# Second attention in program order on TensorE: conv steps between its parts, half of the values' products behind the transposes, both halves copied by ACT

## Chip, core and metric

The kernel runs on one core of a Trainium2 chip. The metric is the device time of one execution in microseconds (us). The engines are TensorE (PE, matrix products; PEld is its weight load), VectorE (DVE), ScalarE (ACT), GpSimd (POOL) and SyncE (SP, which here only issues DMAs). Each engine runs its own queue of instructions in order; semaphores tie the queues together.

## The reference

Two layers on x of shape 2 x 256 x 64 x 64, each with a group norm ahead of it and a residual sum. Layer 0 is an attention with 8 heads over all 4096 positions. Layer 1 is a two-stage block attention plus a 3 x 3 convolution. The part of layer 1 that matters here is its second attention with the sum of both branches:

```
qx = _bn_relu(_c1x1(_bn_relu(_c1x1(feats, fq1_w), ...), fq2_w), ...)
kx = _bn_relu(_c1x1(_bn_relu(_c1x1(feats, fk1_w), ...), fk2_w), ...)
vx = _c1x1(feats, fv_w)
ctx2 = _sa(qx, kx, vx, 8, 8)          # softmax over the 64 positions of a block, 64 blocks
feats2 = _bn_relu(_c1x1(ctx2, sr_W_w), ...)
out = x + rate1 * feats2 + rate2 * conv3x3(...)
```

`_c1x1` is a product with a 256 x 256 matrix over channels, `_bn_relu` a scale and shift per channel with a relu.

## The kernel before, in words

Everything is float32. The two images (b = 0, 1) go one after the other through four stages: projection of layer 0, its attention, the first block attention of layer 1 (tiles named _lr), and `layer1_second`: the second block attention (tiles named _sr) with the convolution woven in. The change is in the last stage and in the helper `group_attention` that the last two share.

An image has NT = 8 tiles of T = 512 positions (8 blocks of 64); its 256 channels are two halves of 128 partitions (KC = 2). For tile t, `layer1_second` does this:

- `branch` for q: two products "ph" (L1075) with relu on ACT into hq (L930), then two products "pr" (`product`, L927) with relu on ACT into rq. The same for k: hk, rk.
- `group_attention`: the scores sp of the 8 blocks (L872), the values vs in two halves of two blocks each (products pvs, L881; half 0 is copied from PSUM by ACT, L886, half 1 by DVE, L888), then the softmax: maximum nm4, difference e, exponential on ACT, sum den, reciprocal and a last multiply (L891 to L898). After a `yield` come two transposes of e into PSUM (at, L903) and two DVE copies into the block-diagonal tile bd (L912); there is one bd for all tiles. After another `yield` come the products pc of vs with bd (L919), handed to ACT for the last relu into res.
- `conv()`, a step of the convolution. There are 16 per image (four strips of 16 rows, four column terms each). A step issues the POOL transform of the *next* step (`conv_transform`: one col, L797, and four v, L801), 16 products into one PSUM tile mm (L811), the ACT copy z of one part of it (L816), four DVE additions that read mm (L817 to L820) and 4 to 12 DVE additions into x (L826 to L838).
- `conv_edges` on DVE (L845), and when a pair of tiles has all its conv steps the final sum with rate1 (L1118) and the store on SP (L1121). Once per image `to_image` copies x into the padded image xp on ACT (L1045), tile by tile ahead of its use, and `fetch_conv_weights` loads the conv weights on SP (L761); for b = 0 it also turns them with 64 transposes (pw, L770), empties the banks with ACT and DVE in turn (L773, L775) and stores them back (L776).

Buffers around the change: PSUM is four banks for all tiles called `bank` and four for the single mm. All work tiles (hq, rq, hk, rk, res, vs, v, z) come from one pool of 11 buffers, given out in the order in which the code asks.

What sets the order: in most stages a scheduler orders each engine's queue by its own estimate, within the data dependences. Inside `with tc.manual_schedule(engines={...})` the named engines keep the order of the program. The first block attention has that for PE; the second does not. There PE's order, as built, is in a steady tile: first piece of ph for q, conv step, rest of ph, pr for q, ph and pr for k, sp and pvs mixed, conv step, at, pc. Each product of 128 x 512 stands in the trace as two pieces ("x8" is four products).

Of the kernel before, what the change touches and what calls it, by code (L numbers as in the profile page):

```python
# [17 lines left out]
P = 128  # L18
B, C, H, W = 2, 256, 64, 64
N = H * W  # L20
T = 512
NT = N // T
KC = C // P
# [8 lines left out]
V_LR, V_FQ1, V_FQ2, V_FK1, V_FK2, V_SRW = (8 + 4 * n for n in range(6))  # L32
# [8 lines left out]
def direct_layers(ctx: ExitStack, tc: tile.TileContext, a: dict, out: bass.AP, bad: bass.AP):  # L41
# [3 lines left out]
    nc = tc.nc  # L45
# [13 lines left out]
    def w4(shape, name, dtype=F32):  # L59
        return work.tile(shape, dtype, tag="w4", name=name)  # L60

    def bank(shape, name):
        return psum["ps"].tile(shape, F32, tag="bank", name=name)
# [29 lines left out]
    for nm, col in (("wk0", V_BK0), ("wq0", V_BQ0)):  # L93
        b0[nm] = const.tile([P, 2], F32, name="b_" + nm)
        for h in range(NH0):
            r = HD0 * (h % 4)
            nc.gpsimd.dma_start(
                out=b0[nm][r : r + HD0, h // 4 : h // 4 + 1],
# [20 lines left out]
    wts = {}  # L119
# [739 lines left out]

    SC1 = C ** -0.5  # L860

    def group_attention(nm, q, k, tokens, wv, out, busy=False):

        sp = bank([P, 4, 64], f"sp_{nm}")
        for t in range(4):
            for c in range(KC):
                for par in range(2):  # L870
                    n0 = (4 * par + t) * 64
                    nc.tensor.matmul(  # L872
                        sp[64 * par : 64 * par + 64, t, :], q[:, c, n0 : n0 + 64], k[:, c, n0 : n0 + 64],
                        start=c == 0, stop=c == KC - 1,
                    )
        vs = w4([P, 4, C], f"vs_{nm}")
        for half in range(2):
            pv = bank([P, 2, C], f"pvs_{nm}_{half}")
            for i in range(2):
                for c in range(KC):  # L880
                    nc.tensor.matmul(  # L881
                        pv[:, i, :], tokens(c, 2 * half + i), wv[:, c, :], start=c == 0, stop=c == KC - 1
                    )
            dst = vs[:, 2 * half : 2 * half + 2, :]
            if half == 0 or busy:
                nc.scalar.copy(dst, pv)  # L886
            else:
                nc.vector.tensor_copy(dst, pv)  # L888

        nm4 = small.tile([P, 4], F32, tag="nm4", name=f"nm4_{nm}")  # L890
        nc.vector.tensor_reduce(nm4, sp, AX.X, ALU.max, negate=True)  # L891
        e = small.tile([P, 4, 64], F32, tag="e", name=f"e_{nm}")
        nc.vector.tensor_tensor(e, sp, nm4.unsqueeze(2).to_broadcast([P, 4, 64]), ALU.add)
        nc.scalar.activation(e, e, AF.Exp, scale=SC1)
        den = small.tile([P, 4], F32, tag="den", name=f"den_{nm}")
        nc.vector.tensor_reduce(den, e, AX.X, ALU.add)
        nc.vector.reciprocal(den, den)
        nc.vector.tensor_tensor(e, e, den.unsqueeze(2).to_broadcast([P, 4, 64]), ALU.mult)  # L898

        yield  # L900
        at = bank([P, 2, 2, 64], f"at_{nm}")
        for u in range(2):
            nc.tensor.transpose(  # L903
                at[:, u].rearrange("p a i -> p (a i)"),
                e[:, 2 * u : 2 * u + 2, :].rearrange("p t j -> p (t j)"), ident,
            )

        bd = bds[turn[0] % 2]
        turn[0] += 1
        for tt in range(2):  # L910
            rows = slice(64 * tt, 64 * tt + 64)
            nc.vector.tensor_copy(  # L912
                bd[rows, :, tt, :].rearrange("p (a u) i -> p u a i", a=2), at[rows]
            )
        yield
        for m in range(KC):
            pc = bank([P, T], f"pc_{nm}_{m}")
            for w in range(4):
                nc.tensor.matmul(  # L919
                    pc[:, w * P : (w + 1) * P], vs[:, w, m * P : (m + 1) * P],  # L920
                    bd[:, w].rearrange("p a i -> p (a i)"), start=True, stop=True,
                )
            out(m, pc)

    def product(pt, wt, src, m, last=True):
        for k in range(KC):
            nc.tensor.matmul(pt, wt[:, k, m * P : (m + 1) * P], src[:, k, :], start=k == 0, stop=last and k == KC - 1)  # L927

    def bn_relu(dst, src, col, m):
        nc.scalar.activation(  # L930
            dst, src, AF.Relu, bias=vecs[:, col + 2 + m : col + 3 + m], scale=vecs[:, col + m : col + m + 1]
        )
# [102 lines left out]
    def layer1_second(b, xts, feats, mean, rstd, shift, pacc):  # L1035

        xp = apool.tile([P, KC, PADW, PADW], F32, tag="A", name=f"xp_{b}")
        for k in range(KC):
            nc.gpsimd.memset(xp[:, k, 0, :], 0.0)
            nc.gpsimd.memset(xp[:, k, PADW - 1, :], 0.0)  # L1040
            nc.gpsimd.memset(xp[:, k, 1 : PADW - 1, 0 : PADW : PADW - 1], 0.0)

        def to_image(t):
            for k in range(KC):
                nc.scalar.activation(  # L1045
                    xp[:, k, 1 + 8 * t : 9 + 8 * t, 1 : 1 + W], xts[t][:, k, :].rearrange("p (r w) -> p r w", w=W),
                    AF.Identity, bias=shift[:, k : k + 1], scale=rstd[:, k : k + 1],
                )

        for t in range(3):  # L1050
            to_image(t)
        results = {}
        turns = [divmod(n, 4) for n in range(4 * NT // 2)]
        ahead = {0: conv_transform(b, xp, *turns[0])}
        done = 0

        def conv():
            nonlocal done
            if done + 1 < len(turns):
                ahead[done + 1] = conv_transform(b, xp, *turns[done + 1])  # L1060
            conv_step(b, xts, wf, ahead.pop(done), *turns[done], pacc)
            done += 1

        for t in range(NT):
            nt = f"sr_{b}_{t}"
            f = [
                feats[k][:, 8 * t : 8 * t + 8].rearrange("p o d e -> p (o d e)") for k in range(KC)
            ]

            def branch(one, two, col1, col2, nm):  # L1070
                hid = w4([P, KC, T], f"h{nm}_{nt}")
                for m in range(KC):
                    ph = bank([P, T], f"ph{nm}_{nt}_{m}")
                    for k in range(KC):
                        nc.tensor.matmul(  # L1075
                            ph, wts[one][:, k, m * P : (m + 1) * P], f[k], start=k == 0, stop=k == KC - 1
                        )
                    bn_relu(hid[:, m, :], ph, col1, m)
                res = w4([P, KC, T], f"r{nm}_{nt}")
                for m in range(KC):  # L1080
                    pr = bank([P, T], f"pr{nm}_{nt}_{m}")
                    product(pr, wts[two], hid, m)
                    bn_relu(res[:, m, :], pr, col2, m)
                return res

            q = branch("fq1", "fq2", V_FQ1, V_FQ2, "q")
            k = branch("fk1", "fk2", V_FK1, V_FK2, "k")
            if t == 0:
                wf = fetch_conv_weights(b)
            for tt in {0: (3, 4)}.get(t, (t + 4,)):  # L1090
                if tt < NT:
                    to_image(tt)
            if t == 0:
                conv()
            res = w4([P, KC, T], f"res_{nt}")

            def to_res(m, pc, res=res):

                bn_relu(
                    res[:, m, :].rearrange("p (d o e) -> p o d e", d=8, o=8),  # L1100
                    pc.rearrange("p (o d e) -> p o d e", o=8, d=8), V_SRW, m,
                )

            parts = group_attention(
                nt, q, k, lambda c, w, f=f: f[c][:, w * P : (w + 1) * P], wts["fv"], to_res
            )
            next(parts)
            conv()
            next(parts)
            if t + 1 < NT:  # L1110
                conv()
            next(parts, None)
            conv_edges(xts, t)
            results[t] = res
            for n in sorted(n for n in results if done >= 4 * (n // 2 + 1)):
                res = results.pop(n)
                for m in range(KC):
                    nc.vector.scalar_tensor_tensor(  # L1118
                        res[:, m, :], res[:, m, :], wts["rate1"], xts[n][:, m, :], ALU.mult, ALU.add
                    )  # L1120
                nc.sync.dma_start(  # L1121
                    out=out[b, :, n * T : (n + 1) * T].rearrange("(k p) n -> p k n", p=P), in_=res
                )
# [583 lines left out]
```

## Time and profile before

| | us |
|---|---|
| median of 3 runs | 3304.72 (3301.09 to 3309.56) |
| the profiled execution | 3297.36, span 3295.2 |
| second attention, image 0, first phq to last pc | 1346.82 to about 1654.2 |
| second attention, image 1, first phq to last pc | 2981.05 to about 3283.7 |
| wait of PE for bd ahead of pc, 16 times | 27.9 in all |

The page gives busy time for each engine, then the span in slices, the chain of work that ended last, and groups of instructions. A group's row reads: line, engine, operation, output <- inputs, shapes, count, busy time, mean time of one, idle time ahead of it and what ended that. A timeline row reads: start, duration, engine, line, operation, output <- inputs, count, and in brackets the idle time ahead of it with its releaser. PE's matmuls are pipelined, so the distance from one start to the next says more than a duration.

### The profile page before, as it was taken

The page shows a single profiled execution, that of the slowest core. Times are in us where ns is not written, and L with a number is a line of the kernel's source. Part 1 is how long each engine was busy: PE and PEld are TensorE (multiplying, and loading weights), DVE is VectorE, ACT ScalarE, POOL GpSimd, SP SyncE. Part 2 cuts the span into 40 slices and gives each one's busy share as a digit, 9 for nine tenths or more (in the row PEclk, how much of TensorE's full clock was granted, in tenths as well). Part 3 has the DMA queues.
Part 4 walks back from the last instruction along what each step waited for, and adds up shares of the span by engine and source line. Part 5 has one row for each costly group of instructions (what it writes and reads, how often), then busy time and mean ns, then how long its engine had stood idle before and what let it go on. Part 6 is the DMA issues. An engine that isn't in the chain of part 4 may idle for free. (4 is left out here: it accounts for less than half of the span.)

```text
span 3295.2 us, 62532 instructions
## 1 busy us (share of the span) xinstructions
PE 3139.2 (95%) x25113; PEld 1844.7 (56%) x25113; DVE 2416.1 (73%) x3138; ACT 2310.7 (70%) x2354; POOL 843.4 (26%) x929
## 2 busy tenths in 40 slices
PE   7999999999999979999979999999999999799998
PEld 4455555555555535666654555555555555356665
DVE  4688888888989888554446887978889898424454
ACT  2798999999989943422227999999999999424222
POOL 2122222223222210444201222222222222005331
PEclk9999999999999979999989999999999999799999
DMA  7967878689776631300159678787797776200000
GB/s 258 251 136 152 168 144 181 145 158 183 143 163 139 141 76 47 134 26 26 45 187 255 137 153 171 142 175 153 158 185 144 156 145 139 79 2 10 14 13 27
DMA packets 243917, 425.23 MB, mean 129 GB/s; under 512 B 99009, under 2 KB 109593, under 8 KB 241185
## 3 DMA queue, kind: packets, MB, share of 16 engines
q0 software_dynamic: 98336, 241.20, 37.8%
q1 hardware_dynamic: 145280, 179.93, 20.5%
q8 instruction: 199, 3.26, 0.4%
q14 instruction: 102, 0.83, 0.1%
HBM read 118.26 MB, written 67.86 MB: 56 GB/s over the span
## 5 line engine op out<-in xcount | busy, mean ns | idle before, releaser
L479 DVE TENSOR_TENSOR e<-e,es 128x1024 f32<-128x1024 f32 (+1 forms) x950 | 1034.4, 1149 | 57.2 <-ACT es L432 57.0
L442 PE MATMUL av<-es,v 128*32 128x256 f32 (+1 forms) x9644 | 745.6, 390 | 0.0
L432 ACT ACTIVATE es<-sa 128x1536 f32<-128x1536 f32 (+1 forms) x444 | 635.6, 1431 | 92.3 <-PE sa L426 47.7
L479 DVE TENSOR_TENSOR e<-e,v 128x1024 f32<-128x1024 f32 (+1 forms) x630 | 668.9, 1118 | 22.7 <-ACT v L432 22.3
L426 PE MATMUL sa<-q,k 128*128 128x512 f32 x1736 | 561.1, 430 | 13.7 <-issue 4.5
L442 PE MATMUL av<-v 128*32 128x256 f32 (+1 forms) x6228 | 506.9, 389 | 0.0
L442 PEld LDWEIGHTS av<-es,v 128*32 128x32 f32 x9644 | 316.2, 109 | 299.4 <-issue 160.2
L426 PEld LDWEIGHTS sa<-q,k 128*128 128x128 f32 x1736 | 279.9, 188 | 297.0 <-issue 139.9
L426 PE MATMUL sc<-q,k 128*128 128x512 f32 x1180 | 373.1, 397 | 7.2 <-ACT es L432 4.3
L426 PE MATMUL sb<-q,k 128*128 128x512 f32 x1180 | 371.3, 396 | 2.1 <-ACT es L432 1.6
L442 PEld LDWEIGHTS av<-v 128*32 128x32 f32 x6228 | 216.3, 109 | 178.5 <-issue 81.5
L432 ACT ACTIVATE es<-sc 128x1024 f32<-128x1024 f32 x296 | 306.8, 1037 | 3.8 <-DVE e L479 3.8
L432 ACT ACTIVATE v<-sc 128x1024 f32<-128x1024 f32 x294 | 304.9, 1037 | 0.4 <-DMA es<-v 0.2
L432 ACT ACTIVATE es<-sb 128x1024 f32<-128x1024 f32 x296 | 302.1, 1021 | 2.9 <-DMA acc<-es 2.9
L432 ACT ACTIVATE v<-sb 128x1024 f32<-128x1024 f32 x294 | 300.1, 1021 | 2.6 <-DMA acc<-v 1.4
L426 PEld LDWEIGHTS sc<-q,k 128*128 128x128 f32 x1180 | 209.0, 187 | 83.6 <-ACT es L432 17.3
L426 PEld LDWEIGHTS sb<-q,k 128*128 128x128 f32 x1180 | 220.2, 188 | 59.0 <-ACT es L432 4.1
L489 POOL DMA_DIRECT2D es<-es x118 | 101.4, 859 | 523.4 <-ACT es L432 468.5
L801 POOL TENSOR_TENSOR v<-col 128x512 f32<-128x512 f32 x128 | 167.0, 1330 | 264.7 <-DMA out_dram<-res_sr 116.9
L432 ACT ACTIVATE v<-sa 128x1536 f32<-128x1536 f32 (+1 forms) x146 | 209.2, 1433 | 33.4 <-PE sa L426 15.2
L811 PE MATMUL mm<-v,wf 128*128 128x256 f32 x1024 | 226.6, 379 | 2.2 <-POOL v L801 1.2
L816 ACT COPY z<-mm 128x512 f32<-128x512 f32 x32 | 18.7, 585 | 283.8 <-PE mm L811 268.3
(241 smaller groups left out, 3519.0 us busy)
## 6 DMA issues: line engine op xcount, KB each, us to landing
acc<-es POOLq DMA_DIRECT2D x122, 512.0 KB, 6.1
acc<-v POOLq DMA_DIRECT2D x76, 512.0 KB, 6.3
es<-es POOLq DMA_DIRECT2D x136, 256.0 KB, 3.8
v<-es POOLq DMA_DIRECT2D x132, 256.0 KB, 4.6
k<-wk_halves SPq DMA_DIRECT2D x64, 512.0 KB
q<-wq_halves SPq DMA_DIRECT2D x256, 128.0 KB
v<-v POOLq DMA_DIRECT2D x92, 256.0 KB, 4.8
es<-v POOLq DMA_DIRECT2D x88, 256.0 KB, 3.8
```

The source lines that it names most:

```text
L426: nc.tensor.matmul(sc[:, i, :], held["k", g // 2][:, j * P : (j + 1) * P], held["q", g, u // 2][:, u % 2, :], start=True, stop=True,)
L432: nc.scalar.activation(dst, sc[:, i : i + m, :], AF.Exp, scale=SC0)
L442: nc.tensor.matmul(dst[HD0 * u : HD0 * u + HD0, n], lhs, rhs(u)[:, n], start=start, stop=stop)
L479: nc.vector.tensor_add(dst[:, s, :], dst[:, s, :], src)
L489: nc.gpsimd.dma_start(out=dst, in_=src, accum_op=ALU.add)
L801: (nc.gpsimd.tensor_add if plus else nc.gpsimd.tensor_sub)(dst, rows(one), rows(two))
L811: nc.tensor.matmul(mm[:, m, r, :], wf[:, k, 4 * r + q, m * P : (m + 1) * P], v[r // 2][:, r % 2, k, :], start=k == 0, stop=k == KC - 1,)
L816: nc.scalar.copy(z[:, 1], mm[:, :, 1, :])
```

## The change

`group_attention` gets a parameter `apart`, set for the second attention alone. With it, half 0 of the values is multiplied ahead of the scores and half 1 behind the transposes and the copies into bd, and ACT copies both. The body of the tile loop goes under `manual_schedule` for PE, in a new order: q branch, image copies, (t = 0: conv weights), conv step, k branch, attention up to the softmax, conv step, transposes with half 1 of the values, pc; at t = 0 a third conv step. In `branch` the second product runs over k outside and m inside, with both banks open.

```
@@ group_attention
+    def group_attention(nm, q, k, tokens, wv, out, busy=False, apart=False):
+        vs = w4([P, 4, C], f"vs_{nm}")
+        def values(half):
+            pv = bank([P, 2, C], f"pvs_{nm}_{half}")
+            for i in range(2):
+                for c in range(KC):
+                    nc.tensor.matmul(
+                        pv[:, i, :], tokens(c, 2 * half + i), wv[:, c, :], start=c == 0, stop=c == KC - 1
+                    )
+            dst = vs[:, 2 * half : 2 * half + 2, :]
+            if half == 0 or busy or apart:
+                nc.scalar.copy(dst, pv)
+            else:
+                nc.vector.tensor_copy(dst, pv)
+        if apart:
+            values(0)
         sp = bank([P, 4, 64], f"sp_{nm}")
...
+        if not apart:
+            values(0)
+            values(1)
...
             nc.vector.tensor_copy(
                 bd[rows, :, tt, :].rearrange("p (a u) i -> p u a i", a=2), at[rows]
             )
+        if apart:
+            values(1)
         yield
@@ layer1_second, branch
+                pr = [bank([P, T], f"pr{nm}_{nt}_{m}") for m in range(KC)]
+                for k in range(KC):
+                    for m in range(KC):
+                        nc.tensor.matmul(
+                            pr[m], wts[two][:, k, m * P : (m + 1) * P], hid[:, k, :], start=k == 0, stop=k == KC - 1
+                        )
                 for m in range(KC):
-                    pr = bank([P, T], f"pr{nm}_{nt}_{m}")
-                    product(pr, wts[two], hid, m)
-                    bn_relu(res[:, m, :], pr, col2, m)
+                    bn_relu(res[:, m, :], pr[m], col2, m)
@@ layer1_second, tile loop
-            q = branch("fq1", "fq2", V_FQ1, V_FQ2, "q")
-            k = branch("fk1", "fk2", V_FK1, V_FK2, "k")
-            if t == 0:
-                wf = fetch_conv_weights(b)
-            for tt in {0: (3, 4)}.get(t, (t + 4,)):
-                if tt < NT:
-                    to_image(tt)
-            if t == 0:
-                conv()
...
-            next(parts)
-            conv()
-            next(parts)
-            if t + 1 < NT:
-                conv()
-            next(parts, None)
+            with tc.manual_schedule(engines={mybir.EngineType.PE}):
+                q = branch("fq1", "fq2", V_FQ1, V_FQ2, "q")
+                for tt in {0: (3, 4)}.get(t, (t + 4,)):
+                    if tt < NT:
+                        to_image(tt)
+                if t == 0:
+                    wf = fetch_conv_weights(b)
+                if t + 1 < NT:
+                    conv()
+                k = branch("fk1", "fk2", V_FK1, V_FK2, "k")
...
+                next(parts)
+                conv()
+                next(parts)
+                next(parts, None)
+                if t == 0:
+                    conv()
```

More of the change, by code (lines that the diff above doesn't have):

```diff
@@ L860, in direct_layers @@
     SC1 = C ** -0.5
-    def group_attention(nm, q, k, tokens, wv, out, busy=False):
+    def group_attention(nm, q, k, tokens, wv, out, busy=False, apart=False):
[14 more added lines that the diff above has]
+            values(0)
         sp = bank([P, 4, 64], f"sp_{nm}")
@@ L875, in group_attention @@
                     )
[L876 to L888, printed above, removed]
+        if not apart:
+            values(0)
+            values(1)
         nm4 = small.tile([P, 4], F32, tag="nm4", name=f"nm4_{nm}")
@@ L1083, in branch @@
-                    bn_relu(res[:, m, :], pr, col2, m)
-                return res
-            q = branch("fq1", "fq2", V_FQ1, V_FQ2, "q")
-            k = branch("fk1", "fk2", V_FK1, V_FK2, "k")
-            if t == 0:
-                wf = fetch_conv_weights(b)
-            for tt in {0: (3, 4)}.get(t, (t + 4,)):
-                if tt < NT:
-                    to_image(tt)
-            if t == 0:
-                conv()
[L1095 to L1102, printed above, removed]
@@ L1104, in layer1_second, with to_res @@
-            parts = group_attention(
-                nt, q, k, lambda c, w, f=f: f[c][:, w * P : (w + 1) * P], wts["fv"], to_res
-            )
-            next(parts)
-            conv()
-            next(parts)
-            if t + 1 < NT:
-                conv()
-            next(parts, None)
+                    bn_relu(res[:, m, :], pr[m], col2, m)
+                return res
+            with tc.manual_schedule(engines={mybir.EngineType.PE}):
[8 more added lines that the diff above has]
+                k = branch("fk1", "fk2", V_FK1, V_FK2, "k")
+                res = w4([P, KC, T], f"res_{nt}")
+                def to_res(m, pc, res=res):
+                    bn_relu(
+                        res[:, m, :].rearrange("p (d o e) -> p o d e", d=8, o=8),
+                        pc.rearrange("p (o d e) -> p o d e", o=8, d=8), V_SRW, m,
+                    )
+                parts = group_attention(
+                    nt, q, k, lambda c, w, f=f: f[c][:, w * P : (w + 1) * P], wts["fv"], to_res, apart=True
+                )
+                next(parts)
+                conv()
+                next(parts)
+                next(parts, None)
+                if t == 0:
+                    conv()
```

## The prediction

> **What bounds the kernel now.** I read the page first: the span and the busy shares.
>
> ```profile
> span 3295.2 us, 62532 instructions
> PE 3139.2 (95%) x25113; PEld 1844.7 (56%) x25113; DVE 2416.1 (73%) x3138; ACT 2310.7 (70%) x2354; POOL 843.4 (26%) x929
> ```
>
> TensorE (PE) is busy 95% of the span; the change touches only the second attention (the _sr tiles), which the slices show twice, at about 1347 to 1655 us (image 0) and 2981 to 3284 us (image 1). So I read that stage alone: the timeline of PE over one tile (columns: start, duration, engine and line, operation, pieces; in brackets idle time and what ended it).
>
> ```profile
> 3022.48 1.02 PE L1075 MATMUL phq_sr<-feats,wt_fq 128*128 128x512 f32 x2
> 3023.34 7.07 PE L811 MATMUL mm<-v,wf 128*128 128x256 f32 x32
> 3030.24 2.74 PE L1075 MATMUL phq_sr<-feats,wt_fq 128*128 128x512 f32 x6
> 3033.16 3.70 PE L927 MATMUL prq_sr<-hq_sr,wt_fq 128*128 128x512 f32 x8 [0.17 <-ACT hq_sr L930]
> 3036.69 3.60 PE L1075 MATMUL phk_sr<-feats,wt_fk 128*128 128x512 f32 x8
> 3040.13 3.88 PE L927 MATMUL prk_sr<-hk_sr,wt_fk 128*128 128x512 f32 x8
> 3043.93 0.34 PE L872 MATMUL sp_sr<-rk_sr,rq_sr 128*64 128x64 f32 x4
> 3044.20 1.13 PE L881 MATMUL pvs_sr<-wt_fv,feats 128*128 128x256 f32 x4
> 3045.26 1.04 PE L872 MATMUL sp_sr<-rk_sr,rq_sr 128*64 128x64 f32 x28
> 3046.22 2.86 PE L881 MATMUL pvs_sr<-wt_fv,feats 128*128 128x256 f32 x12
> 3048.92 7.07 PE L811 MATMUL mm<-v,wf 128*128 128x256 f32 x32
> 3055.82 0.38 PE L903 MATMUL at_sr<-ident,e_sr 128*128 128x128 f32 x2
> 3057.94 2.02 PE L919 MATMUL pc_sr<-bd,vs_sr 128*128 128x128 f32 x16 [1.73 <-DVE bd L912]
> ```
>
> Nothing ends later than PE here: a tile takes 37.32 us (pc to pc), in which DVE is busy 18.2, ACT 9.5 and POOL 14.9 us (busy time by stretch). The chain of waits has the same lines. What is not work on PE is the bracket before pc: after the transposes (at) nothing is queued, and PE waits until DVE has copied them to bd. Smaller losses show only as starts further apart than the same work elsewhere: phk takes 3.44 from start to start, but phq 0.86+2.92, prq 3.53, prk 3.80, and sp with pvs 4.99 instead of 1.08+3.56 (at 3003.39 us).
>
> **What the Trainium skill says.** "Perfetto Trace Analysis", Optimizing DMA Performance, Optimization Strategies: keep the matmul engine busy by working on whatever blocks it; the trace agrees that this engine blocks here. "SBUF — State Buffer", Who interferes with whom: a DVE instruction with two SBUF inputs and a GpSimd (POOL) instruction that reads SBUF exclude each other, the later one blocks. The trace agrees:
>
> ```profile
> 3007.11 7.35 DVE L832 SCALAR_TENSOR_TENSOR x<-z,edges,x 128x128 f32<-128x128 f32 x7
> L832 DVE SCALAR_TENSOR_TENSOR x<-z,edges,x x128: 334/345/2297, 1378.8 to 3249.4; 128x128 f32<-128x128 f32 x128
> ```
>
> Seven additions took 7.35 us while POOL ran v transforms, against a median of 345 ns alone. "TensorE: Matmul & The Clock Gate", What's actually happening: the clock falls after an idle window of about 3.4 us. The gaps here are 1.7 us, and the granted clock reads 1.00 in the tile, so I book no gain in clock.
>
> **The change part by part.** One tile of dense PE work, by starts: phq, prq, phk, prk 4 x 3.44 = 13.76; two conv steps 2 x 6.90 = 13.80; sp 1.08; pvs 3.56; at 0.28 (as at 2948.30 us, where work follows it); pc 1.86; sum 34.34. Now it is 37.32, so 2.98 is loss: 1.84 between at and pc, 0.34 phq, 0.09 prq, 0.36 prk, 0.35 sp with pvs. The new order on PE, read from the built program, is phq, prq, conv A, phk, prk, pvs half 0, sp, conv B, at, pvs half 1, pc. From phq = 0: prq 3.44, conv A 6.88, phk 13.78, prk 17.22, pvs 20.66, sp 22.44, conv B 23.52, at 30.42, pvs 30.70, pc due 32.48.
> - *Values behind the transposes.* bd took 2.12 us from at to pc, with one z addition between its two copies; DVE keeps that order. at and four pieces of values fill 0.28+1.78 = 2.06 of it. But pc's third block needs half 1: its last piece ends 2.22 after at's start, ACT copies from 2.34 (0.12 later, as at 3122.03) for 0.585, PE resumes 0.15 later, at 3.08. pc starts at 2.12, does two blocks (0.46) and waits from 2.58 to 3.08. With 0.06 at its start the new wait is 0.56 (bounds 0 and 1.0). Queued behind it on PE: the rest of pc, then the next phq; on ACT the copy stands behind conv B's z copy (0.585, begins 0.2 after at) and before res.
> - *Both halves on ACT.* 0.59 more on ACT (9.5 of 37 us busy), 0.68 less on DVE (18.2): hidden in their idle time.
> - *pr with k outermost.* The first two pieces need only the first half of hq or hk, one more 1.72 us later; hq half 0 is ready at 2.7 (ACT: two res until 1.0, hq from 1.9), prq is due at 3.44. In the old order hq stood behind z and two res. The 0.34 and 0.09 go.
> - *pvs half 0 ahead of sp.* rk half 1 is ready at about 21.6, sp comes at 22.44: the 0.36 and 0.35 go.
> - *Conv A ahead of k.* A conv step issues 5 POOL, 1 ACT and about 4 + 4 to 12 DVE instructions. SP's and POOL's order is unchanged; v's buffers come free elsewhere (from hq, rq, rk, v and res), on my reading at 6.9, 10.4 or 23.5 of the tile before, and POOL needs 7.4 us, so in the steady tiles v is over 20 us early. The single PSUM tile of mm is free about 4.2 us after a conv step (at starts 3130.46, L820 ends 3134.67); 9.7 or more lie between, once (third step of an image) 5.3. At risk is the softmax: DVE must finish conv A's additions first. z starts at 14.6, four reads of mm make it 17.3, 4 to 12 additions 20.8 to 22.6; sp ends at 23.52. The chain from maximum to e is 3.07 us (3120.97 to 3124.04), plus 1.28 if a POOL v blocks its last multiply (two SBUF inputs; POOL's v starts when sp ends): done at 27.9, at is due at 30.42. I take 0; bounds 0 and 1.0 in a tile.
> - *First tiles.* Image 0: the 64 transposes of the conv weights (7.0 us) come before k. Their 4096 KB load is over by 1356 (DMA share 0.00 from there); prq ends at 1355.1. But ACT empties every second bank, and from 1352.2 on has four image copies, two rq and three more image copies (0.73 and 0.76 each) before it, to 1358.8: PE stalls after the fifth bank, 2.3 us (bounds 0 and 3). The store of the weights follows and is waited for by nobody near. hq's wait stays: 1.3 (image 0), 0.7 (image 1).
>
> Sum from first phq to last at. Image 1: 8 x 20.54 + 16 x 6.90 - 3.92 (at to pc of the last tile) = 270.8; + 7 x 0.56 + 0.7 = 275.4; before 3279.72 - 2981.05 = 298.7; gain 23.3. Image 0: 270.8 + 3.9 + 7.0 + 1.3 + 2.3 = 285.3; before 1650.22 - 1346.82 = 303.4; gain 18.1. What follows at in both (additions, store, and in image 0 load, statistics, projection) hangs on the last conv step and moves along. Together 41.4: 3295.2 becomes 3253.8 in the profiled execution; the median, 9.5 above that span, becomes 3304.7 - 41.4 = 3263.
>
> **Rivals.**
> - *Only the bd wait goes.* If hq and rk waits return at the new places, 1.84 - 0.56 = 1.28 in each of 16 tiles: 20.5 us, 3284. For: ACT's queue is in order and has one more copy. Against: the ready times above.
> - *Image 0's gain is lost.* If the projection of image 1 waited for a load not tied to the stage's end: only 23.3, 3281. Against: DVE waits there for the last x tile (4.97 us), which is loaded after the stage.
> - *The softmax comes late* (slower). If POOL's transforms lie beside conv A's additions in every tile, these take 1.05 us (L832, 7.35/7), 1.76 (the long L838 at 3108.61) and 1.38 (the longest L1118): in every second tile 8 x 1.05 + 4 x 1.76 = 15.4 from 17.3 on, so nm at 32.7 and e at 37.1, 6.7 late; in the others 4 x 1.76 + 2 x 1.38 + 0.9 = 10.7, e at 32.4, 2.0 late. A mean of 4.35 less the gain of 2.42 is +1.9 a tile, +31: 3336. It decides from 2.4 us a tile. Against: POOL's buffers come free at sp's end, so its v runs from 23.5 on and not beside the additions.
> - *The change doesn't do what it says*: excluded, the order is in the program.
>
> **How the numbers follow.** Forecast 3263: 0.75, its own range 3254 to 3274 (0 to 1.0 us at pc in 14 tiles, 0 to 3 for the banks, and the runs before spread 8.5 us). Only the bd wait 0.12; image 0 lost 0.05; softmax late 0.05; no visible change 0.03. The range 3254 to 3284 takes in the first three. About 0.3% (10 us) is what a measurement can tell from no change: faster 0.92, same 0.03, slower 0.05.
>
> **What would show it.** Right: tiles of 34.9 us; the bracket before pc at or below 0.1 with a second one of about 0.5 inside pc that ACT's vs ends; no brackets before prq and sp; a stall of some 2 us after the fifth bank of pw. Wrong: a wait of at for e (DVE's additions stretched beside POOL), of mm for v, or of sp for rk.

## The result, and the profile after

| | before | after |
|---|---|---|
| median | 3304.91 us (4 runs, 3301.09 to 3309.56) | 3262.14 us (4 runs, 3257.70 to 3265.94) |
| ratio | | 0.9869, 95% interval 0.9851 to 0.9888 |
| second attention, image 0, first phq to last at | 303.40 | 284.22 |
| second attention, image 1, first phq to last at | 298.67 | 274.77 |
| one steady tile | 37.32 | 34.78 |

The changed kernel is 1.3% faster. The page's first lines of the kernel after, span and busy shares:

```profile
span 3259.0 us, 62523 instructions
PE 3129.8 (96%) x25113; PEld 1845.7 (57%) x25113; DVE 2394.0 (73%) x3122; ACT 2327.3 (71%) x2370; POOL 837.0 (26%) x929
```

PE does the same 25113 pieces. DVE has 16 instructions fewer and ACT 16 more: the copies of half 1, one for each tile. The page says no more; the stage does. The timeline of PE over one tile of the kernel after (start, duration, operation, pieces, and in brackets the idle time with its releaser):

```profile
3045.91 3.60 PE L1084 MATMUL phq_sr<-feats,wt_fq 128*128 128x512 f32 x8
3049.34 3.60 PE L1092 MATMUL prq_sr<-hq_sr,wt_fq 128*128 128x512 f32 x8
3052.78 7.07 PE L811 MATMUL mm<-v,wf 128*128 128x256 f32 x32
3059.68 3.60 PE L1084 MATMUL phk_sr<-feats,wt_fk 128*128 128x512 f32 x8
3063.12 3.60 PE L1092 MATMUL prk_sr<-hk_sr,wt_fk 128*128 128x512 f32 x8
3066.55 1.89 PE L873 MATMUL pvs_sr<-wt_fv,feats 128*128 128x256 f32 x8
3068.37 1.15 PE L890 MATMUL sp_sr<-rk_sr,rq_sr 128*64 128x64 f32 x32
3069.45 7.17 PE L811 MATMUL mm<-v,wf 128*128 128x256 f32 x32
3076.46 0.38 PE L910 MATMUL at_sr<-ident,e_sr 128*128 128x128 f32 x2
3076.68 1.89 PE L873 MATMUL pvs_sr<-wt_fv,feats 128*128 128x256 f32 x8
3078.63 2.22 PE L928 MATMUL pc_sr<-bd,vs_sr 128*128 128x128 f32 x16
```

There is no bracket left. phq, prq, phk and prk each take 3.43 from start to start, the first half of the values with sp 2.90. The only row that differs from dense work is pc: the next phq starts at 3080.69, so pc takes 2.06 instead of the 1.86 it had before. Those 0.20 are the wait for half 1, too short inside a row to get a bracket of its own.

The waits of PE over the stage of image 1 in the kernel after (total, times, longest):

```profile
PE phq_sr L1084 <- ACT feats L939: 1.3, 1, 1.3
PE prq_sr L1092 <- ACT hq_sr L939: 0.4, 1, 0.4
```

In the kernel before there are five: 13.8 for bd in eight tiles, 1.9 for e, 1.3 for feats, 1.2 for v and 1.2 for hq. What is left stands at the stage's first tile.

The last multiply of the softmax on DVE, in this tile of the kernel after:

```profile
3071.60 0.95 DVE L905 TENSOR_TENSOR e_sr<-e_sr,den_sr 128x256 f32<-128x256 f32 x1
```

e is done at 3072.55 and the transposes come at 3076.46: 3.9 us to spare.

The two stages gain 19.2 and 23.9, 43.1 together; the medians differ by 42.8. The profiled spans differ by only 36.2, because stretches that the change doesn't touch differ between executions: the first phq came at 1346.8 before and 1350.5 after, and from the last at of image 0 to the first phq of image 1 it was 1330.8 and 1334.0. Over the profiles of all experiments these two range from 1347.1 to 1355.7 and from 1331.6 to 1338.8, with no tie to the edits. So the experiments are read by tile and stage, and the medians beside them.

### The profile page after: what moved, and what is told of

Its sections match the earlier page's. It is cut to its first block, busy times and chain, and to the rows that moved or that the text cites. A ratio compares the mean times of both kernels' runs of the same rounds, so it can differ in the third digit from the quotient of the medians.

```text
span 3259.0 us, 62523 instructions
## 1 busy us (share of the span) xinstructions
PE 3129.8 (96%) x25113; PEld 1845.7 (57%) x25113; DVE 2394.0 (73%) x3122; ACT 2327.3 (71%) x2370; POOL 837.0 (26%) x929
## 5 line engine op out<-in xcount | busy, mean ns | idle before, releaser
L811 PEld LDWEIGHTS mm<-v,wf 128*128 128x128 f32 x1024 | 193.2, 190 | 33.1 <-issue 7.2
```

What stands on the lines that cost most here:

```text
L811: nc.tensor.matmul(mm[:, m, r, :], wf[:, k, 4 * r + q, m * P : (m + 1) * P], v[r // 2][:, r % 2, k, :], start=k == 0, stop=k == KC - 1,)
```

## The experiments

All tiles and stages are of the profiled executions; "image 0" and "image 1" are distances from the first phq to the last at. Edits are on the kernel after, if nothing else is said.

| kernel | steady tile | image 0 | image 1 | median | ratio to before, 95% |
|---|---|---|---|---|---|
| before + split values | 35.24 | 286.99 | 282.38 | 3272.35 | 0.9907 (0.9890 to 0.9923) |
| the same + pr's loops | 34.96 | 285.02 | 280.48 | 3269.05 | 0.9893 (0.9876 to 0.9910) |
| values together | 36.31 | 296.62 | 287.18 | 3283.45 | 0.9945 (0.9932 to 0.9959) |
| pr with m outside | 35.34 | 288.50 | 278.95 | 3267.87 | 0.9892 (0.9877 to 0.9908) |
| half 1 copied by DVE | 40.4 to 41.5 | 329.36 | 319.70 | 3352.81 | 1.0148 (1.0134 to 1.0162) |
| conv A ahead of pc | 36.8 or 38.5 | 304.71 | 295.51 | 3298.45 | 0.9984 (0.9977 to 0.9991) |
| softmax 3.2 later | 35.62 | 287.55 | 282.93 | 3271.79 | 0.9901 (0.9885 to 0.9916) |
| scheduler orders PE | 34.58 | 282.80 | 274.74 | 3258.35 | 0.9873 (0.9858 to 0.9888) |
| weights behind the scores | 34.78 | 282.63 | 274.78 | 3260.89 | 0.9871 (0.9856 to 0.9886) |
| pc by halves | 34.58 | 282.80 | 273.34 | 3256.14 | 0.9856 (0.9841 to 0.9871) |
| the last two together | 34.58 | 281.16 | 273.28 | 3254.80 | 0.9849 (0.9834 to 0.9864) |

### The values put back together

```
         if apart:
             values(0)
+            values(1)
...
-        if apart:
-            values(1)
```

> Only the values go back together: both halves are multiplied ahead of the scores, both still copied by ACT; the conv steps and pr keep their new places. Theory (the values behind the transposes fill PE's wait for bd): at to pc falls from 0.28 + 1.78 of work with a 0.2 stall to 0.28 of work and the old wait; the bracket before pc is back at 1.7 to 1.9, ended by DVE's bd, the tile goes from 34.8 to 36.4, and 16 tiles cost 25 us: 3287. Rival (the gain comes from the places of the conv steps and from PE's written-out order, and the values are only one of several fillers): tile below 35.1, 3262 to 3267.

PE in one tile of this kernel:

```profile
3091.29 0.38 PE L911 MATMUL at_sr<-ident,e_sr 128*128 128x128 f32 x2
3093.46 2.02 PE L927 MATMUL pc_sr<-bd,vs_sr 128*128 128x128 f32 x16 [1.79 <-DVE bd L920]
```

From at to pc it is 2.17, exactly what the kernel after needs with 1.78 of work in it. The half of the values now takes its 1.73 ahead of the scores and the wait at pc is as long as if it were still there; pc's stall of 0.20 for half 1 goes. Together that is the 1.53 a tile by which 36.31 exceeds 34.78, and it comes to 24.8 us in the two stages and 21 in the median. The rival falls: nothing else of the change fills that wait.

### The split alone, on the kernel before

`group_attention` of the kernel after in the kernel before; conv steps, pr and the scheduler unchanged.

```
-                nt, q, k, lambda c, w, f=f: f[c][:, w * P : (w + 1) * P], wts["fv"], to_res
+                nt, q, k, lambda c, w, f=f: f[c][:, w * P : (w + 1) * P], wts["fv"], to_res, apart=True
```

> The kernel before with one part of the change alone: half of the values behind the transposes, both copied by ACT. The conv steps, pr and the scheduler stay as before; as built, PE does conv A after the first piece of phq, and pc by halves of the values. Theory (this part alone is worth its terms of the sum): the wait for bd of 1.84 goes with no stall for half 1, and the 0.35 of sp mixed with pvs goes, the waits of 0.34, 0.09 and 0.36 for hq and hk stay: 2.1 to 2.2 a tile, 33 to 35 us, 3270 to 3272. Rival (the conv step's place is needed too, because in the old place z, two res and hq crowd ACT ahead of the vs copies): below 1.3 a tile, 3284 or more.

PE in one tile of this kernel, behind the conv step at its start:

```profile
3090.47 2.74 PE L1084 MATMUL phq_sr<-feats,wt_fq 128*128 128x512 f32 x6
3093.38 3.70 PE L936 MATMUL prq_sr<-hq_sr,wt_fq 128*128 128x512 f32 x8 [0.18 <-ACT hq_sr L939]
3096.92 3.60 PE L1084 MATMUL phk_sr<-feats,wt_fk 128*128 128x512 f32 x8
3100.36 3.87 PE L936 MATMUL prk_sr<-hk_sr,wt_fk 128*128 128x512 f32 x8
```

bd's bracket is gone, and this part is worth 2.08 a tile, where the whole change brings 2.54. (The scheduler takes pc by halves of the values here, so the 0.20 for half 1 is not in it.) What is left shows in the starts: 2.91 from the rest of phq to prq (2.58 dense), 3.54 for prq, 3.71 for prk, whose successor starts at 3104.07 (3.43 dense).

### The split and pr's loops, on the kernel before

```
-                    pr = bank([P, T], f"pr{nm}_{nt}_{m}")
-                    product(pr, wts[two], hid, m)
+                pr = [bank([P, T], f"pr{nm}_{nt}_{m}") for m in range(KC)]
+                for k in range(KC):
+                    for m in range(KC):
+                        nc.tensor.matmul(
+                            pr[m], wts[two][:, k, m * P : (m + 1) * P], hid[:, k, :], start=k == 0, stop=k == KC - 1
+                        )
```

> The kernel before with two parts of the change: the values split around the transposes, and pr with k outermost. The conv step stays after the first piece of phq, the scheduler orders PE. From the run with the split alone (tile 35.24: phq with its wait 2.92 after the conv step, prq 3.53, prk 3.71). Theory (k outermost hides the second halves only; hq half 0 stands on ACT behind z and two res as long as the conv step lies at the tile's start): prk goes from 3.71 to 3.43 and prq from 3.53 to 3.43, the 0.34 ahead of prq stays: tile 34.86, 3266, and moving the conv step away is worth the remaining 0.28 to the 34.58 of the run with pc by halves. Rival (k outermost alone removes all waits for hq and hk, the conv step's move buys nothing): tile 34.5 to 34.6, 3261 or less.

PE in one tile of this kernel:

```profile
3088.69 2.74 PE L1084 MATMUL phq_sr<-feats,wt_fq 128*128 128x512 f32 x6
3091.60 3.70 PE L1092 MATMUL prq_sr<-hq_sr,wt_fq 128*128 128x512 f32 x8 [0.17 <-ACT hq_sr L939]
3095.14 3.60 PE L1084 MATMUL phk_sr<-feats,wt_fk 128*128 128x512 f32 x8
3098.57 3.60 PE L1092 MATMUL prk_sr<-hk_sr,wt_fk 128*128 128x512 f32 x8
```

prk is dense (3098.57 to 3102.01), but the wait of prq stays to the last digit, in its second half too (3.54): with the conv step at the tile's start, the loops don't remove it. So moving the conv step is worth the 0.38 from 34.96 to the 34.58 of the run with pc by halves. It is worth more in the first tile of image 1: there the old places leave waits of 1.2 for v, 1.0 for the PSUM tile of mm and 2.5 for e, and the stage is 7.1 longer than with pc by halves, of which 7 x 0.38 = 2.7 are the steady tiles.

### pr with m outside

```
-                for k in range(KC):
-                    for m in range(KC):
+                for m in range(KC):
+                    for k in range(KC):
```

> Only the loops of the second product are swapped back: m outside, k inside, both banks open as before. Theory (k outermost hides half 1 of hq and hk): the second product of m = 0 then needs half 1 at 0.86 after pr's start instead of 1.72; half 1 is ready about 1.0 to 1.05 after pr's start (0.12 to the relu, 0.73 for it, 0.15 to PE), so each of the two pr of a tile waits 0.15 to 0.2: 0.3 to 0.4 a tile, 5 to 6 us: 3268. Rival (the hq and hk waits came from the relus' place in ACT's queue and went with the conv step): below 0.1 a tile, 3262 to 3264.

PE in one tile of this kernel:

```profile
3058.59 3.87 PE L1092 MATMUL prq_sr<-hq_sr,wt_fq 128*128 128x512 f32 x8
3062.30 7.07 PE L811 MATMUL mm<-v,wf 128*128 128x256 f32 x32
```

ACT in the same tile, the relu of half 1 of hq:

```profile
3058.79 0.78 ACT L939 ACTIVATE hq_sr<-phq_sr,vecs 128x512 f32<-128x512 f32 x1 [0.88 <-PE phq_sr L1084]
```

The relu for half 1 starts 0.20 after prq and ends 0.98 after it; with m outside, PE needs it at 0.86. Each pr takes 3.71 instead of 3.43: 0.28 twice, 0.56 a tile where 0.3 to 0.4 were expected. The mechanism is the expected one. The relu starts 0.08 later and takes 0.05 longer than assumed, and PE goes on 0.16 after its end, as assumed. So with the conv step moved the loops are worth 0.56 a tile, twice what they are worth with it at the tile's start (35.24 less 34.96).

### Half 1 copied by DVE

```
-            if half == 0 or busy or apart:
+            if half == 0 or busy:
```

> Half 1 of the values is copied by DVE instead of ACT; nothing else. In DVE's queue the copy stands behind the four reads of mm and the additions into x of conv B (4 to 12 of them). Theory (the place in the queue decides, and the copy on ACT is needed for the gain): from at on DVE does bd, z, bd, three z and 8 x additions of 0.34 to 0.42 each, until 6.3 after at, then the copy of 0.69; pc's third block, due 2.6 after at, resumes at 7.1: 4.5 a tile in the steady tiles, some 65 us in all, 3327, slower than before. Rival (the engine is of no matter, as the prediction's hidden copies would suggest): 0 to 0.2 a tile, 3262 to 3265.

DVE in one tile of this kernel:

```profile
1450.04 1.92 DVE L832 SCALAR_TENSOR_TENSOR x<-z,edges,x 128x128 f32<-128x128 f32 x7
1451.88 0.68 DVE L880 COPY vs_sr<-pvs_sr 128x512 f32<-128x512 f32 x1
```

PE in the same tile:

```profile
1445.93 0.38 PE L910 MATMUL at_sr<-ident,e_sr 128*128 128x128 f32 x2
...
1448.10 0.68 PE L928 MATMUL pc_sr<-bd,vs_sr 128*128 128x128 f32 x4
1452.62 2.93 PE L928 MATMUL pc_sr<-bd,vs_sr 128*128 128x128 f32 x12 [3.84 <-DVE vs_sr L880]
1455.34 4.70 PE L1084 MATMUL phq_sr<-feats,wt_fq 128*128 128x512 f32 x8
```

The copy stands behind all of the conv step's additions, and pc waits 3.84 or 4.42 in the steady tiles. One word in the program turns a gain of 43 us into a loss of 50 (the kernel before took 3302.36 beside it). That is more than the 4.5 a tile that were expected: 6.4 (44.9 over 7 tiles). The rest is in the last two rows: 12 pieces of pc take 2.72 to the next start instead of some 1.4, and phq 4.54 instead of 3.43. The granted clock, the share of TensorE's full clock that the trace says was granted, was 0.50 in the stretch from 1452.60 to 1455.34. So part of the loss is the wait and part the slower PE behind it.

### Conv A between the values and pc

```
-                if t + 1 < NT:
+                if t == 0:
                     conv()
...
                 next(parts)
+                if t + 1 < NT:
+                    conv()
                 next(parts, None)
-                if t == 0:
-                    conv()
```

> Conv A is moved from ahead of the k branch to between the second half of the values and pc, 2.06 behind conv B on PE; the rest stays. Theory (the steps must lie apart because mm is one PSUM tile, free again about 4.3 us after a step's last product): conv A waits 2.3 for mm, in which PE has nothing; pc's own stall of 0.2 goes. 2.1 in each of 14 tiles: 29 us, 3291, with a bracket of 2.3 before the second conv step of a tile. Rival (any work between the transposes and pc does, where the steps lie is of no matter): pc's stall goes and nothing comes, 3259.

PE in two tiles of this kernel:

```profile
3064.40 8.83 PE L811 MATMUL mm<-v,wf 128*128 128x256 f32 x32 [2.25 <-DVE z L820]
...
3102.86 7.14 PE L811 MATMUL mm<-v,wf 128*128 128x256 f32 x32 [2.25 <-DVE z L820]
```

The waits and the starts of the same conv steps as stretches (length, busy time and instructions of PE, PEld, DVE, ACT, POOL, then granted clock, DMA share, GB/s):

```profile
3061.47:3064.88 3.41, 1.16 (x6) 0.73 (x5) 3.35 (x9) 0.59 (x1) 0.00 (x0) 1.00 0.00 0
3064.88:3068.29 3.41, 3.41 (x9) 2.70 (x9) 1.98 (x6) 0.00 (x0) 0.00 (x0) 0.50 0.13 52
3099.01:3102.43 3.42, 1.60 (x8) 1.07 (x6) 3.36 (x7) 0.86 (x2) 0.00 (x0) 1.00 0.00 0
3102.43:3105.84 3.41, 2.98 (x14) 2.67 (x15) 3.39 (x12) 0.00 (x0) 0.00 (x0) 1.00 0.03 7
```

The wait for the one PSUM tile of mm is there in all 14 tiles, 2.25 to 2.30, against the 2.3 expected: conv steps have to lie apart. But the loss was 41.2 in the two stages, not 29. In 8 of the 14 tiles the conv step behind the wait took 8.71 to 8.83 instead of 7.14, because the granted clock was 0.50 for 3.41 us: 8 x 1.65 is 13 us more. In the other 6 it took 7.14 behind the same wait, and the clock did not fall.

The trace shows what parts the two groups. The eight falls lie whole multiples of 3.413 us apart; in image 1 they begin at 3027.33, 3064.88, 3139.97 and 3215.07. Cut the stage at these times and at every 3.413 us between them. Then the stretch ahead of each fall has 2.01 to 2.30 of idle PE, as in the first row (3.41 less 1.16 is 2.25). In the other six tiles a border divides the wait, and no stretch has more than 1.82 idle, as in the third row.

### The softmax 3.2 us later

DVE takes the maximum of the scores eight times; the result is the same maximum.

```
-        nc.vector.tensor_reduce(nm4, sp, AX.X, ALU.max, negate=True)
+        for _ in range(8 if apart else 1):
+            nc.vector.tensor_reduce(nm4, sp, AX.X, ALU.max, negate=True)
```

> The kernel after with DVE taking the maximum of the scores eight times instead of once in each tile of the second attention, seven maxima of 0.45 more: e comes 3.2 us later; nothing else changes. Theory (the softmax has 3.9 us to spare in the kernel after, its last multiply ends at 3072.55 and the transposes are due at 3076.46): tile stays at 34.78 in image 1; in image 0, where two statistics instructions stand among the maxima in every second tile, up to 1 us in 3 tiles; 3262 to 3266. Rival (the spare time is not there, because DVE gives it back in what follows or POOL's transform stretches the maxima): a wait of at for e in most tiles, 1 to 3 a tile, 3278 or more.

PE at the transposes of one tile of this kernel:

```profile
3091.41 0.44 PE L911 MATMUL at_sr<-ident,e_sr 128*128 128x128 f32 x2 [0.62 <-DVE e_sr L906]
```

DVE in the same tile:

```profile
3083.73 3.63 DVE L899 TENSOR_REDUCE nm_sr<-sp_sr 128x4 f32<-128x256 f32 x8 [2.97 <-PE sp_sr L890]
...
3088.97 2.38 DVE L906 TENSOR_TENSOR e_sr<-e_sr,den_sr 128x256 f32<-128x256 f32 x1
```

POOL in the same tile:

```profile
3083.93 4.92 POOL L801 TENSOR_TENSOR v<-col 128x512 f32<-128x512 f32 x4 [10.71 <-PE sp_sr L890]
3088.93 2.14 POOL L797 TENSOR_TENSOR col<-xp 128x1152 f32<-128x1152 f32 x1
```

The maxima took the expected time, but the last multiply, 0.42 when alone, took 2.38: it came 0.04 after POOL had begun col and ended 0.28 after col did. In the kernel after the same multiply meets a short v and takes 0.95. The delay of 3.2 and the 1.43 more of the block are 4.6, 0.7 over the 3.9 of the timeline, and at comes 7.80 after conv B's start instead of 7.01. In the kernel after col begins 3.4 behind the multiply's start (3074.98), so a delay of 3.2 is about the first to meet it; smaller ones were not tried. Neither theory holds: the delay was not free, and at 9.7 us in the median and 11.5 in the two stages it cost less than the rival's 1 to 3 a tile. Ten of the 16 tiles waited at at. Nine waited about 0.6 and took up to 0.84 longer; the first tile of image 1 waited 2.29, and the granted clock fell behind that wait.

### Without the written order, and pc by halves

The first edit takes `with tc.manual_schedule` away from the tile loop (its body stays in the same order). As built the steady tile's order is the same, only pc is taken by halves. The second keeps the written order and changes pc alone:

```
-        for m in range(KC):
-            pc = bank([P, T], f"pc_{nm}_{m}")
-            for w in range(4):
+        pcs = [bank([P, T], f"pc_{nm}_{m}") for m in range(KC)]
+        for ws, m in ((range(2), 0), (range(2), 1), (range(2, 4), 0), (range(2, 4), 1)) if apart else ((range(4), 0), (range(4), 1)):
+            for w in ws:
...
-            out(m, pc)
+            if 3 in ws:
+                out(m, pcs[m])
```

> The written-out order of PE in the second attention is dropped; the program text stays, the scheduler orders PE. As built it gives the same order in the steady tile but for pc, whose products it takes by halves of the values: blocks 0 and 1 of both banks, then 2 and 3. Theory (the order of the program and the split of the values do it, the manual order itself is worth nothing, and the 0.2 stall in pc is the wait for half 1): pc is due for half 1 0.46 later, the stall is gone, tile 34.55, and 3258 to 3262. Rival (the manual order is what buys the gain): 3275 or more.

> Only pc's products are reordered: blocks 0 and 1 (half 0 of the values) for both banks first, then blocks 2 and 3. Theory (pc stalls 0.2 a tile for half 1): half 1 is due 0.46 later, the stall goes: tile 34.58, 16 x 0.2 = 3.2 us less, 3259. Rival (the 0.2 is a wait for bd or an effect of the weight loads): tile stays at 34.78, 3262.

PE in one tile of the kernel with pc by halves:

```profile
3105.90 2.02 PE L928 MATMUL pc_sr<-bd,vs_sr 128*128 128x128 f32 x16
3107.76 3.60 PE L1085 MATMUL phq_sr<-feats,wt_fq 128*128 128x512 f32 x8
```

pc is back at 1.86 and the tile at 34.58 in both runs: the 0.20 was the wait for half 1, and the written order itself is worth nothing in the steady tile: with pc taken alike, the tile is 34.58 with it and without it. In the first tile of image 1 the scheduler puts four pieces of the conv step between phq and prq, where they wait 1.2 for v; that is why its image 1 is 1.4 longer. The medians of the two, 3258.35 and 3256.14, have intervals that overlap each other's and that of the kernel after.

### The weights' transposes behind the scores

```
-                if t == 0:
-                    wf = fetch_conv_weights(b)
-                if t + 1 < NT:
+                if t > 0:
                     conv()
...
                 next(parts)
+                if t == 0:
+                    wf = fetch_conv_weights(b)
                 conv()
```

> In tile 0 of each image the first conv step, and for image 0 the transposes of the conv weights with it, are moved behind the scores; the missing step is done in the last tile, ahead of its k branch. Theory from the trace after (PE waited 1.2 to 1.5 us for the load of the conv weights ahead of pw): the load is over long before pw then; image 0's stage, first phq to last at, is 284.2 - 1.6 = 282.6, image 1's unchanged at 274.8; 3260 to 3261. Theory of the prediction (PE stalls in pw because ACT has image copies ahead of its evictions): pw's stall stays if image copies or relus still lie in ACT's queue there, at most 0.35 is saved: 284. Rival: the softmax of tile 0 now lies beside the evictions and at waits for it: image 0 longer by up to 2.

PE in the first tile of image 0 in the kernel after:

```profile
1355.25 3.70 PE L1092 MATMUL prq_sr<-hq_sr,wt_fq 128*128 128x512 f32 x8 [1.08 <-ACT hq_sr L939]
1360.18 7.51 PE L770 MATMUL pw<-ident,wf 128*128 128x128 f32 x64 [1.23 <-DMA wf<-wf_kept]
1367.53 7.07 PE L811 MATMUL mm<-v,wf 128*128 128x256 f32 x32
```

PE in the same tile of this kernel:

```profile
1366.10 1.15 PE L890 MATMUL sp_sr<-rk_sr,rq_sr 128*64 128x64 f32 x32
1367.19 7.42 PE L770 MATMUL pw<-ident,wf 128*128 128x128 f32 x64
```

The bracket for the load is gone, and image 0 is 282.63, as the first theory said to 0.03. But this run takes pw away from the load and from ACT's image copies at once (the last of them ends at 1361.5, ahead of pw), so by itself it doesn't tell the two causes apart. The other profiles do. PE in the first tile of image 0 in the kernel with pc by halves, where prq starts at 1351.92:

```profile
1356.30 2.40 PE L770 MATMUL pw<-ident,wf 128*128 128x128 f32 x20 [0.68 <-DMA wf<-wf_kept]
1359.34 5.02 PE L770 MATMUL pw<-ident,wf 128*128 128x128 f32 x44 [0.64 <-ACT wf L773]
1364.20 7.07 PE L811 MATMUL mm<-v,wf 128*128 128x256 f32 x32
```

Here the load was waited for less, and pw stopped again after its fifth bank until ACT had emptied one. The conv step behind pw starts 12.28 after prq, exactly as in the kernel after. Seven profiles with pw in this place show both waits (0.62 to 0.87 for the load, 0.46 to 0.69 for ACT), and in all seven the conv step starts 12.27 to 12.39 after prq: what one wait takes less, the other takes more. What stays the same is ACT: its image copies follow one another without a pause, and its first copy of pw begins 6.76 to 6.89 after prq, in the kernel after too. So ACT's image copies set the time, as the prediction held. The wait for the load lies ahead of theirs and, at 0.62 to 1.23, cost nothing of its own, although its bracket is the only one that the kernel after shows at pw. This is read from the profiles; no run moved the image copies alone.

### Both together

> Both edits together: pc by halves of the values, and the weights' transposes with the first conv step behind the scores in tile 0. The two savings lie in different places, so they add: 3.2 + 1.6 = 4.8 us less than after, 3257 to 3258. If one of them only moves a wait, half of that.

Image 0 is 3.1 shorter than in the kernel after, image 1 1.5: together 4.55 of the 4.8 expected. The median, 3254.80, is the lowest of all, but its interval overlaps that of the kernel after, so the gain over it rests on the stages of the profiles.

## Why the prediction was right

**The sum.** 3263 was predicted and 3262.14 measured. Image 1 was to take 275.4 and took 274.8, image 0 285.3 and took 284.2; the tile 34.9 and took 34.78. That the medians agree to 1 us is luck in part, since the four runs spread over 8.2. So is the nearness of the tile: from phq to at it took 30.55 instead of 30.42, from at to the next phq 4.23 instead of 4.48, and the two errors have opposite signs.

**Values behind the transposes.** Right in kind: the wait for bd goes, a shorter one for half 1 comes, inside pc and from ACT. The new wait was mis-sized: 0.56 predicted, 0.26 measured (0.06 at pc's start, 0.20 for half 1; from at to the next phq 4.23, not 4.48). ACT's copy began 2.15 after at, not 2.34, since the values started 0.22 after at and ACT followed their end by 0.04. Conv B took back 0.11: 7.01 from its start to at, not 6.90.

**Both halves on ACT.** Hidden, as predicted. The prediction saw no more in it than that; the run with the copy on DVE shows that without it the change loses more than it gains.

**pr with k outermost, pvs ahead of sp, conv A ahead of k.** Together right, wrongly shared out. The prediction let the loops remove the 0.34 and 0.09 ahead of prq and inside it, and the place of pvs the 0.36 of prk. The runs on the kernel before show it otherwise: the wait at prq goes only with the conv step (0.38, with pr's second half), and 0.28 of prk's 0.36 is the loops' work. Nor does the conv step's place do it alone: with m outside again, prq and prk lose 0.28 each. Removed step by step, a tile goes 37.32, 35.24 (split), 34.96 (loops), 34.58 (conv A), and 34.78 with pc by banks.

**First tiles.** In image 0 the cause was right and its size too large. PE sat idle for 1.31 at pw (1.23 ahead of it and, too short for a bracket, 0.08 inside) where 2.3 were predicted; ACT's first copy of pw began 6.76 after prq instead of the 7.2 that the prediction's times give (1358.8 less 1351.6). The sign that it named, a stall of some 2 us after the fifth bank, did not come in the kernel after, because PE stood most of that time ahead of pw, waiting for the load. That the load "is over by 1356" was read from the kernel before. In the kernel after it was waited for until 1360.18, with the stage begun 3.65 later; this error cost the sum nothing, since ACT's copies ended later still.

In image 1's first tile the old order had waits of 1.9 for e and 1.2 for v that the prediction never named, and between the wait for e and the one for bd behind it the granted clock fell (at 3018.85). PE there in the kernel before:

```profile
3017.02 0.44 PE L903 MATMUL at_sr<-ident,e_sr 128*128 128x128 f32 x2 [1.92 <-DVE e_sr L898]
3019.11 3.53 PE L919 MATMUL pc_sr<-bd,vs_sr 128*128 128x128 f32 x16 [1.66 <-DVE bd L912]
```

The next phq starts at 3022.48, so this pc took 3.37 instead of 1.86, at a granted clock of 0.53. The prediction read a clock of 1.00 in the tile after this one and booked no gain; here were 1.5 us of it. The two waits and the clock are in its total all the same, because it built the new stage up from dense work and subtracted it from the old one, instead of adding up the tile's losses.

**The rivals.** Only the bd wait: no bracket for hq or rk came back in the steady tiles. Image 0's gain lost: it gained 19.2. The softmax late: not in this order, e was 3.9 early. Its mechanism is real, though: the Trainium skill, "SBUF — State Buffer", SBUF: two separate sides, says that of a DVE instruction with two SBUF inputs and a GpSimd (POOL) one that reads SBUF, the one that starts first has the shared ports for its whole instruction and the other blocks. The run with the later softmax agrees, with a 0.42 multiply that took 2.38 beside a col of 2.14. There it decided at 3.2 us of delay, although the timeline had shown 3.9 to spare. The seven additions of 7.35 that the prediction read as lying beside v transforms lay beside a col too, which POOL ran for 2.14 from 3011.64.

## What to carry to other kernels

Where PE waits for another engine to turn its own result around, put work there that is due right afterwards, and look at once at who has to hand that work on: here the copy was free on ACT's queue and cost 6.4 us a tile on DVE's, behind additions that nobody waited for. Build the new order up from dense work and compare stages, not spans: stretches that an edit doesn't touch differed by up to 9 us between executions. A bracket names what ended one wait, not what that wait costs: compare when the next work starts, as behind pw, where a shorter wait for the load only made room for a longer one for ACT. Spare time read from a timeline holds for the order it was read from; a later start can meet another engine's longer instruction.

## What the runs showed of the hardware

- TensorE's granted clock fell behind 8 of 14 waits of 2.25 to 2.30 us (conv A ahead of pc), to 0.50 for 3.41 us each time, while 16 waits of 1.8 in the kernel with the values together cost nothing. What parted the falls from the rest was the idle time within one stretch of 3.413 us, as worked out beside that run. Over the two stages of all thirteen traces, cut the same way, the clock fell behind each of the 24 stretches with 1.89 or more of idle PE that began at full clock, and behind none with 1.82 or less, so a little over half of a stretch was enough there. Outside these stages the border is less sharp: the lowest idle time with a fall is 1.57, the highest without one 1.99. The Trainium skill, "TensorE: Matmul & The Clock Gate", What's actually happening, has the clock fall after an idle window of about 3.4 us; these waits were shorter, and the measurement decides.
- One DVE multiply with two SBUF inputs took 0.42 alone, 0.95 beside a POOL transform of v and 2.38 beside the longer col. The kernel after does this multiply 16 times. Twelve of them started while POOL was in a v or a col, and each took what was left of POOL's instruction (0.59 to 0.93) and 0.28 or 0.29 more; the other four took 0.42 or 0.43. The 2.38 is the same sum: 2.10 was left, and it ended 0.28 after col.
